# State space stage of a Macaron kernel: one transfer per repeated tile, and one overlapping read for the four shifted copies

## The chip, the cores and the metric

The kernel runs on one core of a Trainium2 chip. The core has TensorE (PE), VectorE (DVE), ScalarE (ACT), GpSimd (POOL) and SyncE (SP); here SP issues every transfer, in its program's order, to a queue that 16 DMA engines serve. Time is device microseconds of one execution. A profiled execution gives the span and the trace; single runs without a profile give the median that is compared.

## The reference

The input is `[16, 512, 256]` in float32: 16 sequences of 512 positions. Two layers follow each other. The first is a feed-forward part with blockwise FP4 rounding, a state space part, and the feed-forward part again. The second is a feed-forward part with a mixture of low-rank experts, causal attention with ALiBi, and the experts again. The change touches the state space part alone:

```python
xz = hidden_states @ W_in                       # 256 -> 2 x 512
x, z = jnp.split(xz, 2, axis=-1)
x = conv(x, conv_w)                             # 4 taps along the sequence, per channel
x = silu(x + conv_b)
proj = x @ W_x                                  # dt_low (16), B (16), C (16)
dt = jax.nn.softplus(dt_low @ W_dt + b_dt)      # 512 channels
A = -jnp.exp(A_log)                             # 512 x 16
...
h = jnp.exp(dt_t[..., None] * A) * h + (dt_t * x_t)[..., None] * B_t[:, None, :]
y = jnp.einsum('bds,bs->bd', h, C_t)
...
y = y + x * D
y = y * silu(z)
out = y @ W_out
```

There are 512 channels with 16 states each, for every sequence: 8192 recurrences of 512 steps.

## The kernel before

Three parts run one after the other: `ffn_phase` on all sequences, `mamba_phase` (the state space stage), then `ffn_phase` again and `attn_phase`. Only `mamba_phase` and its weights are touched.

**One scan.** VectorE runs the recurrence with one scan instruction (line 975) over a tile of 128 partitions by 2 x 512 elements. A partition is a pair of channel and state: 32 channels times 4 states, and the two halves of the free dimension are two further groups of 32 channels. So a sequence takes 32 scans: `where(t)` gives `b` (sequence), `c` (block of 128 channels, 0 to 3) and `k` (0 to 7, of which `k // 2` is one of four groups of states, `q`, and `k % 2` the half `p` of the channels). Each scan needs `da = exp(dt * A)` (ScalarE, `factors`), `bx = dt*u * B` (GpSimd, `make_bx`; for `q = 2` TensorE makes it instead, `turn_bx`), and after it `g = h * C` (VectorE or GpSimd), which TensorE sums over the states into `y` (`accumulate`).

**Repeated tiles.** `dt` and `dt*u` are made once per channel, on 128 partitions of channels, but the scans want each channel on four partitions (one for each state of a group), and `B` and `C` on 32 (one for each channel). This repetition is done through DRAM:

- `to_dtu` (line 762) writes the tile `dt` (dt and dt*u, two blocks of channels) to DRAM as `dd`. `fetch_steps(b, c)` (line 562) reads it back as two tiles `ds` (p = 0, 1), each 128 partitions by 2 x 2 x 512, in four transfers of 32 partitions, one for each repetition. `ds` has four buffers.
- `proj` holds B and C; two transfers (line 745) write them to DRAM as `bd`. `fetch(b, q)` (line 549) fills a tile `bc` with four transfers, each of which repeats one row of `bd` on 32 partitions.

**Shifted copies.** The convolution is done by TensorE from a stack `xs` of 128 partitions: four copies of 32 channels, each shifted by one more position. `to_xp` (line 661) copies the projected block to `xp`, stores it to DRAM as `xc` (line 679), and fills the stack with four transfers of 32 partitions, one for each tap, each with its own offset (line 682). The first three columns of the stacks were set to zero once (line 521). `taps(c)` (line 649) is the product that reads the stack. The first sequence does its convolution on VectorE, without a stack.

**Order.** `prepare(b + 1)` is a generator for all that the next sequence needs (projection, convolution, B, C, dt). The loop over `t` (line 959) runs a scan and its surrounding work and then advances `prepare` by one step, so the next sequence is prepared between the scans of the running one. Instructions of the compute engines in this stage are kept in program order (`keep_in_program_order`), so one that waits holds all that stand behind it on its engine. Fetches for the next block or sequence are issued at fixed places by `k` and `c` (lines 1012 to 1028).

## Time and profile before

| | us |
|---|---|
| median of 3 runs | 4369.89 (4368.17 to 4375.62) |
| profiled execution, its own time | 4368.95 |
| its span | 4367.2 |
| VectorE busy, whole span | 3630.1 (83%) |
| TensorE busy, whole span | 3748.3 (86%) |
| GpSimd busy, whole span | 1844.2 (42%) |

The DMA view lists the transfers by source and size; these are the ones that the change touches, with the median time from issue to landing:

| transfer | count | KB each | us to landing |
|---|---|---|---|
| `ds<-dd` | 512 | 256 | 6.5 |
| `xs<-xc` | 240 | 256 | 4.7 |
| `bc<-bd` | 256 | 128 | 6.3 |
| `dd<-dt` | 32 | 1024 | 4.7 |
| `xc<-xp` | 60 | 256 | 3.5 |

How to read it: a busy share over the whole span mixes stages with different limits, so the state space stage has to be read by itself, from windows of time. A transfer's time to landing includes its wait in the queue behind others that were issued before. "Released by" in a list of waits is the event that came last.

### The profile page before, as it was taken

Reading aid. Unit: us, or ns where it says so; the run is one execution under the profiler, and the core shown is the slowest. Engines: PE = TensorE matmul, PEld = TensorE weight load, DVE = VectorE, ACT = ScalarE, POOL = GpSimd, SP = SyncE. Lnnn points to the kernel's source line nnn. Section 1 sums busy time; section 2 is a strip of 40 time slices with the busy share of each in tenths; the row PEclk is TensorE's granted clock in tenths of the full one; section 3 lists DMA queues with packets and bytes.
Section 4 is the critical chain, followed back from the end, with each engine's and each line's share of the span. In section 5 each row is a group of like instructions: output and inputs, shape, how many; then the busy total and the mean of one; then the engine's idle time right before and its main releaser. Section 6 shows DMA issues by size and latency. Waiting matters only on the chain.

```text
span 4367.2 us, 68836 instructions
## 1 busy us (share of the span) xinstructions
PE 3748.3 (86%) x26498; PEld 2068.1 (47%) x26498; DVE 3630.1 (83%) x5002; ACT 2317.5 (53%) x3546; POOL 1844.2 (42%) x1687
## 2 busy tenths in 40 slices
PE   7999966777777777777777779999999999999989
PEld 4666632333333233333333346666764555555547
DVE  9999837887788888887878979999877888888876
ACT  4444336666666667766666634443534444444444
POOL 1000027888788788888888920000211111111122
PEclk9999978889888888898888889999999999999999
DMA  4000035667776666666677520000000000000002
GB/s 140 15 15 20 15 93 140 160 164 167 176 173 158 156 159 162 163 164 160 159 174 173 131 107 1 1 1 1 13 20 16 16 21 18 19 15 20 18 13 68
DMA packets 165786, 371.32 MB, mean 85 GB/s; under 512 B 37633, under 2 KB 57666, under 8 KB 165458
## 3 DMA queue, kind: packets, MB, share of 16 engines
q1 hardware_dynamic: 165458, 366.93, 33.3%
q8 instruction: 208, 3.41, 0.3%
q14 instruction: 120, 0.98, 0.1%
HBM read 272.18 MB, written 77.86 MB: 80 GB/s over the span
## 4 chain that ended last, share of the span: by engine, by line
PE 60%; DVE 15%; ACT 9%; DMA 9%; issue 3%; POOL 2%; SPq 2%; DVEq 0%; ACTq 0%; POOLq 0%
PE s L1192 10%; PE g L288 7%; PE u L288 7%; PE o L324 7%; DVE h L975 6%; DMA ds<-dd 5%; PE p L491 5%; PE p L1192 4%; PE y L491 4%; ACT da L482 3%; PE p L1195 3%; PE o L1192 3%; DMA xc<-xp 3%; PE da L491 2%; PE o L491 2%
## 5 line engine op out<-in xcount | busy, mean ns | idle before, releaser
L485 POOL TENSOR_TENSOR bx<-ds,bc 128x1024 f32<-128x1024 f32 x384 | 900.0, 2361 | 258.3 <-DMA ds<-dd 203.7
L482 ACT ACTIVATE da<-ds,a_neg 128x511 f32<-128x511 f32 x768 | 528.2, 689 | 285.4 <-DMA ds<-dd 103.8
L491 PE MATMUL y<-g,fold 128*32 128x512 f32 x2048 | 406.4, 673 | 185.0 <-DVE g L488 147.8
L485 POOL TENSOR_TENSOR g<-hs,bc 128x1024 f32<-128x1024 f32 x224 | 527.3, 2365 | 83.9 <-DVE hs L975 81.7
L975 DVE TENSOR_TENSOR_SCAN hs<-da,bx 128x1024 f32<-128x1024 f32 x224 | 508.1, 2279 | 65.6 <-POOL bx L485 65.1
L1363 ACT ACTIVATE eT<-s 128x768 f32<-128x768 f32 (+1 forms) x384 | 338.3, 881 | 420.9 <-PE s L1192 420.9
L1369 POOL TENSOR_SCALAR_AFFINE_SELECT eT<-eT 128x256 f32<-128x256 f32 (+1 forms) x384 | 189.0, 492 | 864.1 <-ACT eT L1363 864.1
L975 DVE TENSOR_TENSOR_SCAN h<-da,bx 128x1024 f32<-128x1024 f32 x160 | 366.8, 2292 | 127.1 <-POOL bx L485 77.9
L1192 PE MATMUL s<-k,q 32*128 32x256 f32 (+3 forms) x2048 | 459.5, 470 | 9.1 <-DVE mx L1323 5.7
L1323 DVE TENSOR_REDUCE mx<-s 128x2 f32<-128x1024 f32 (+3 forms) x512 | 410.2, 822 | 12.5
L975 DVE TENSOR_TENSOR_SCAN h<-ds,da 128x1024 f32<-128x1024 f32 x128 | 293.8, 2296 | 150.7 <-PE da L491 87.3
L1192 PE MATMUL s<-qm,k 32*128 32x512 f32 (+3 forms) x2048 | 385.7, 471 | 17.8 <-ACT eT L1363 11.4
L488 DVE TENSOR_TENSOR g<-h,bc 128x1024 f32<-128x1024 f32 x288 | 350.8, 1218 | 15.6 <-issue 0.4
L491 PE MATMUL p<-xT,w_in 128*128 128x512 f32 x500 | 293.9, 717 | 58.7 <-ACT dT L482 33.8
L1319 DVE TENSOR_TENSOR s<-s,mask 128x256 f32<-128x256 f32 (+1 forms) x384 | 198.8, 518 | 154.3 <-PE s L1192 143.9
L293 ACT ACTIVATE sl<-g 128x352 f32<-128x352 f32 x256 | 118.4, 464 | 384.9 <-PE g L288 373.7
L1192 PEld LDWEIGHTS s<-k,q 32*128 32x128 f32 x2048 | 206.3, 185 | 171.2 <-issue 93.6
L1520 POOL TENSOR_TENSOR g<-rs,v 128x4 f32<-128x4 f32 x64 | 13.1, 209 | 636.8 <-ACT rs L1517 549.4
L491 PEld LDWEIGHTS y<-g,fold 128*32 128x32 f32 x2048 | 60.5, 114 | 444.5 <-DVE g L488 253.9
L491 PE MATMUL da<-diag,dT 128*32 128x128 f32 x8192 | 247.8, 275 | 4.6 <-DVE hs L975 4.4
L491 PEld LDWEIGHTS da<-diag,dT 128*32 128x32 f32 x8192 | 217.8, 110 | 68.3 <-issue 45.2
L514 POOL MEMSET ds<- 128x2 f32 x2 | 0.1, 101 | 532.9 <-DMA xd<-x 532.9
(286 smaller groups left out, 7777.8 us busy)
## 6 DMA issues: line engine op xcount, KB each, us to landing
ds<-dd SPq DMA_DIRECT2D x512, 256.0 KB, 6.5
xs<-xc SPq DMA_DIRECT2D x240, 256.0 KB, 4.7
bc<-bd SPq DMA_DIRECT2D x256, 128.0 KB, 6.3
dd<-dt SPq DMA_DIRECT2D x32, 1024.0 KB, 4.7
xc<-xp SPq DMA_DIRECT2D x60, 256.0 KB, 3.5
x<-_attn_hidden_states_dram SPq DMA_DIRECT2D x16, 512.0 KB, 7.1
xd<-x SPq DMA_DIRECT2D x16, 512.0 KB, 2.6
xo<-xd SPq DMA_DIRECT2D x16, 512.0 KB, 3.7
```

Of the source, the lines that this page charges most:

```text
L288: nc.tensor.matmul(dst, lhsT=xT[:, k, c * P : (c + 1) * P], rhs=w[:, k, f0 : f0 + HF], start=(k == 0), stop=(k == KD - 1),)
L324: last = nc.tensor.matmul(o, lhsT=hT[:, f, :], rhs=wdT[:, f, :], start=(f == 0), stop=False)
L482: return tc.keep_in_program_order(nc.scalar.activation(out, in_, func, **kw))
L485: tc.keep_in_program_order(nc.gpsimd.tensor_tensor(out, in0, in1, op=op))
L488: tc.keep_in_program_order(nc.vector.tensor_tensor(out, in0, in1, op=op))
L491: tc.keep_in_program_order(nc.tensor.matmul(out, **kw))
L975: tc.keep_in_program_order(nc.vector.tensor_tensor_scan(flat(h), flat(da[t % 2]), flat(bx[t % 2] if turned else bx.pop(t)), 0.0, op0=ALU.m ...
L1192: tc.keep_in_program_order(nc.tensor.matmul(out, **kw))
L1319: nc.vector.tensor_tensor(own, own, const["mask"][:, :w].unsqueeze(1).to_broadcast([P, 2, w]), op=ALU.add)
L1323: nc.vector.tensor_reduce(mx[:, t, 2 * pair : 2 * pair + 2, RM], s[:, :, off : off + (t + 1) * P], axis=AX.X, op=ALU.max,)
L1363: const["exp"] = nc.scalar.activation(eT[:, 2 * pair : 2 * pair + 2, e0 : e0 + w], s[:, :, :w], AF.Exp)
L1369: nc.gpsimd.affine_select(out=own, in_=own, compare_op=ALU.is_ge, fill=0.0, base=0, pattern=[[0, 2], [0, n], [1, P]] if n > 1 else [[0, 2] ...
```

## The change

- `xp` gets three more columns on its left (`XS` = 515), set to zero once, so that `xc` in DRAM holds each channel's row with its zeros in front; `xc` is laid out with the channel `m` outermost and the four groups `i` next to each other.
- The stack is filled by one transfer, whose source is an access pattern written by hand: four copies, each starting one element later, of 32 rows of 2057 elements that run over all four groups. The stacks need no zeros of their own.
- `dd` is laid out by `[j, p, m, g, x, s]`, so that all that one `ds` tile needs of a channel is one run of 2048 elements. `to_dtu` writes it with four transfers of 64 partitions. A `ds` tile is filled by one transfer with the repetition of four as the outermost dimension of its source.
- A `bc` tile is filled by one transfer of four rows, each repeated 32 times.
- The transfers that fill the stack and that write `dd` are put on a list (`later`) and issued at the next step of the loop (`run_later`); the places of the fetches by `k` and `c` are written anew.

The instructions on SP, as built, per sequence: `ds` 8 where there were 32, `bc` 4 for 16, `xs` 4 for 16, `dd` 8 for 2. The access patterns as built (step and count of each dimension, outermost first):

```
ds  out [2048,128][1,1][1,2048]   in [0,4][2048,32][1,2048]      before: out [2048,32][1024,2][1,1024]  in [1024,32][32768,2][1,1024]
bc  out [1024,128][1,1][1,1024]   in [4096,4][0,32][1,1024]      before: out [1024,32][1,1024]          in [0,32][1,1024]
xs  out [2060,128][1,1][1,2057]   in [1,4][2060,32][1,2057]      before: out [2060,32][515,4][1,512]    in [512,32][16384,4][1,512]
xc  out [515,4][2060,32][1,515]   in [515,128][1,1][1,515]       before: out [512,128][1,512]           in [512,128][1,512]
dd  out [1024,2][2048,32][1,1024] in [2048,64][1,1][1,1024]      before: out [1024,128][131072,2][1,1024] in [2048,128][1024,2][1,1024]
```

```diff
+XS = SEQ + DCONV - 1
...
-            w["xp"].append(mw.tile([P, SEQ], F32, name=f"xp{i}"))
+            xp = mw.tile([P, XS], F32, name=f"xp{i}")
+            nc.gpsimd.memset(xp[:, : DCONV - 1], 0.0)
+            w["xp"].append(xp)
...
-                t = m1.tile([P, 4, SEQ + DCONV - 1], F32, name=f"xs{i}")
-                nc.gpsimd.memset(t[:, :, : DCONV - 1], 0.0)
-                stacks.append(t)
+                stacks.append(m1.tile([P, 4, XS], F32, name=f"xs{i}"))
...
-                    for i in range(4):
-                        n = 4 * i + q
-                        nc.sync.dma_start(
-                            out=bc[32 * i : 32 * i + 32],
-                            in_=bds[b][n : n + 1].to_broadcast([32, 2, SEQ]),
-                        )
-                        yield
+                    nc.sync.dma_start(
+                        out=bc,
+                        in_=bds[b].rearrange("(i q) x s -> q i (x s)", i=4)[q]
+                        .unsqueeze(1).to_broadcast([4, 32, 2 * SEQ]),
+                    )
...
-                        for i in range(4):
-                            nc.sync.dma_start(
-                                out=t[32 * i : 32 * i + 32],
-                                in_=rows_of[:, 2 * p : 2 * p + 2],
-                            )
-                            yield
+                        nc.sync.dma_start(
+                            out=t,
+                            in_=steps_of[b, c // 2][c % 2, p]
+                            .rearrange("m g x s -> m (g x s)")
+                            .unsqueeze(0).to_broadcast([4, 32, 4 * SEQ]),
+                        )
+                        yield
...
-                    act(xp, p, AF.Copy)
-                    xc = md.tile([4, 32, SEQ], F32, name="xc", tag="xc", bufs=4)
-                    nc.sync.dma_start(out=xc.rearrange("i m s -> (i m) s"), in_=xp)
-                    for k in range(DCONV):
-                        o = DCONV - 1 - k
+                    act(xp[:, DCONV - 1 :], p, AF.Copy)
+                    xc = md.tile([32, 4, XS], F32, name="xc", tag="xc", bufs=4)
+                    nc.sync.dma_start(out=xc.rearrange("m i s -> i m s"), in_=xp)
+
+                    def spread_x():
+                        n = 4 * XS - DCONV + 1
                         nc.sync.dma_start(
-                            out=stacks[c % 2][32 * k : 32 * k + 32, :, o : o + SEQ],
-                            in_=xc.rearrange("i m s -> m i s"),
-                        )
+                            out=stacks[c % 2].rearrange("p i s -> p (i s)")[:, :n],
+                            in_=bass.AP(
+                                xc.tensor, xc.offset, [[1, DCONV], [4 * XS, 32], [1, n]]
+                            ),
+                        )
+
+                    later.append(spread_x)
...
-                    dd = md.tile([2, P, 2, SEQ], F32, name="dd", tag="dd", bufs=4)
-                    nc.sync.dma_start(out=dd.rearrange("j p x s -> p j x s"), in_=t)
+                    dd = md.tile([2, 2, 32, 2, 2, SEQ], F32, name="dd", tag="dd", bufs=4)
                     steps_of[b, h] = dd
+
+                    def store():
+                        for j in range(2):
+                            for p in range(2):
+                                nc.sync.dma_start(
+                                    out=dd[j, p].rearrange("m g x s -> g m (x s)"),
+                                    in_=t[64 * p : 64 * p + 64, j],
+                                )
+
+                    later.append(store)
...
+            def run_later():
+                for do in later:
+                    do()
+                later.clear()
...
+                run_later()
                 for _ in range(2 if t < 8 or s in (24, 26, 28, 30) else 1):
                     next(rest if t < 4 else ahead, None)
...
+                if b and s == 0:
+                    fetch(b, NQ - 1)
+                if k == (0, 0, 0, 2)[c]:
+                    steps = fetch_steps(*divmod(b * NDC + c + 1, NDC))
+                    next(steps, None)
+                if k == (1, 3, 2, 3)[c]:
+                    next(steps, None)
                 if c == NDC - 1 and k in (2, 4, 6):
-                    for _ in fetch(b + 1, k // 2 - 1):
-                        pass
-                if b and s == 0:
-                    for _ in fetch(b, NQ - 1):
-                        pass
+                    fetch(b + 1, k // 2 - 1)
```

More of the change, by code (lines that the diff above doesn't have):

```diff
@@ L519, in mamba_phase @@
             for i in range(2):
-                t = m1.tile([P, 4, SEQ + DCONV - 1], F32, name=f"xs{i}")
-                nc.gpsimd.memset(t[:, :, : DCONV - 1], 0.0)
-                stacks.append(t)
+                stacks.append(m1.tile([P, 4, XS], F32, name=f"xs{i}"))
             state, xns, xos, zss, rows, norms, bds = {}, {}, {}, {}, {}, {}, {}
-            spread, steps_of = {}, {}
+            spread, steps_of, later = {}, {}, []
             h0 = ps_h.tile([P, 2, SEQ], F32, name="h", tag="h")
@@ L553, in fetch @@
                     rows[b, q] = bc
-                    for i in range(4):
-                        n = 4 * i + q
-                        nc.sync.dma_start(
-                            out=bc[32 * i : 32 * i + 32],
-                            in_=bds[b][n : n + 1].to_broadcast([32, 2, SEQ]),
-                        )
-                        yield
+                    nc.sync.dma_start(
[3 more added lines that the diff above has]
+                    )
             def fetch_steps(b, c):
                 if b < NB:
-                    rows_of = steps_of[b, c // 2][c % 2].rearrange(
-                        "(g m) x s -> m g x s", m=32
-                    )
                     for p in range(2):
@@ L932, in mamba_phase @@
                     break
-            for _ in itertools.chain(
-                fetch_steps(0, 0), *(fetch(0, q) for q in range(NQ))
-            ):
-                pass
+            run_later()
+            for _ in fetch_steps(0, 0):
+                pass
+            for q in range(NQ):
+                fetch(0, q)
             spare.clear()
@@ L991, in mamba_phase @@
                     next(stat, None)
+                run_later()
                 for _ in range(2 if t < 8 or s in (24, 26, 28, 30) else 1):
@@ L1011, in mamba_phase @@
                     finish_mult(*done.pop())
-                if c == NDC - 1 and k in (2, 4, 6):
-                    for _ in fetch(b + 1, k // 2 - 1):
-                        pass
-                if b and s == 0:
-                    for _ in fetch(b, NQ - 1):
-                        pass
-                if c < NDC - 1:
-                    if k == 0:
-                        steps = fetch_steps(b, c + 1)
-                    for _ in range((4, 0, 0, 2, 2, 1)[k] if k < 6 else 0):
-                        next(steps, None)
-                else:
-                    if k == 2:
-                        steps = fetch_steps(b + 1, 0)
-                    if k in (2, 3, 4, 5):
-                        next(steps, None)
-                        next(steps, None)
+                if b and s == 0:
[5 more added lines that the diff above has]
+                    next(steps, None)
+                if c == NDC - 1 and k in (2, 4, 6):
+                    fetch(b + 1, k // 2 - 1)
                 if s == STEPS - 1:
```

## The prediction

> **What bounds the kernel now.** I first read the page's slices, to place the stage that changes. The rows are forty equal slices of 109 us.
>
> ```profile
> DMA  4000035667776666666677520000000000000002
> GB/s 140 15 15 20 15 93 140 160 164 167 176 173 158 156 159 162 163 164 160 159 174 173 131 107 1 1 1 1 13 20 16 16 21 18 19 15 20 18 13 68
> ```
>
> The state space stage is the stretch from slice 5 to slice 23, the only one where transfers are busy for long. Next came the table of windows, cut into stretches of 120.8 us, which is the distance between equal points of neighbouring sequences (one sequence of 512 is 32 scans). Columns: busy time of each engine, granted clock, share of the 16 DMA engines that is busy, GB/s.
>
> ```profile
> core 0: us, PE busy (x) PEld busy (x) DVE busy (x) ACT busy (x) POOL busy (x), PEclk, DMA share, GB/s
> 820.80:941.60 120.80, 91.14 (x832) 38.92 (x830) 99.11 (x73) 81.31 (x115) 98.70 (x58) 0.87 0.68 169
> 941.60:1062.40 120.80, 91.75 (x832) 38.84 (x826) 100.07 (x72) 83.31 (x117) 97.94 (x57) 0.92 0.68 166
> 1062.40:1183.20 120.80, 91.01 (x818) 38.73 (x816) 96.67 (x70) 79.88 (x112) 97.97 (x57) 0.86 0.66 161
> ```
>
> VectorE and GpSimd carry some 99 us of the 121, TensorE 91; the DMA engines rest for a third, about 40 us. No engine is full, so I read the chain of waits over the stage (607 to 2545 us), where the transfers show:
>
> ```profile
> by line: DVE h L975 12.9%; DMA ds<-dd 11.6%; PE p L491 11.4%; PE y L491 8.4%; ACT da L482 7.3%; DMA xc<-xp 5.7%; PE da L491 5.4%; issue 4.3%; DVE g L488 3.8%; PE o L491 3.7%; DVE hs L975 3.4%; ACT L482 3.1%; SPq L682 1.9%; ACT zs L482 1.5%;
> ```
>
> Of 1938 us, `ds<-dd` holds 225, `xc<-xp` 110 and SP's issuing of `xs` 37: transfers already sit on the path, so how fast they run decides. For that I read the DMA view in four short windows. In order: `xs` and `ds` (1031.1 to 1040.2 us); `ds` and `bc` (1106.7 to 1133.5); one `dd<-dt` store (1214.8 to 1217.7); reloads of whole x tiles (2570.2 to 2572.2).
>
> ```profile
> DMA packets 815, 1.84 MB, mean 202 GB/s; under 512 B 111, under 2 KB 111, under 8 KB 815
> q1 hardware_dynamic: 815, 1.84, 96.0%
> ...
> DMA packets 1921, 6.05 MB, mean 226 GB/s; under 512 B 448, under 2 KB 448, under 8 KB 1919
> q1 hardware_dynamic: 1919, 6.03, 94.6%
> ...
> DMA packets 272, 1.05 MB, mean 362 GB/s; under 512 B 16, under 2 KB 16, under 8 KB 272
> q1 hardware_dynamic: 272, 1.05, 90.2%
> ...
> DMA packets 215, 0.82 MB, mean 408 GB/s; under 512 B 16, under 2 KB 16, under 8 KB 215
> q1 hardware_dynamic: 215, 0.82, 99.9%
> ```
>
> The percentage is the busy share of sixteen engines, so the rate of one busy engine follows. Loads into 32 partitions: 202/(16 x 0.960) = 13.2 and 226/(16 x 0.946) = 14.9 GB/s, together about 14. The store from 128 partitions: 362/(16 x 0.902) = 25.1. Loads into 128 partitions: 408/16 = 25.5. One more thing is in the third row: 272 packets, 16 of them tiny, for 128 rows of two 4 KB pieces, so 256 and one closing packet for each of 16 engines. Every large transfer of this trace has an outermost count of 128 or 32, which deals out evenly to 16.
>
> **The change, part by part.** The instructions of TensorE, VectorE and ScalarE, and their order, stay the same. Only SP's queue changes, and two memsets of GpSimd (110 ns each), which move ahead of the stage into work on weights; they count as nothing, and 0.2 us without that cover.
>
> Issues on SP, per sequence: `ds` 32 to 8, `bc` 16 to 4, `xs` 16 to 4, `dd` 2 to 8, so 42 fewer. At 0.43 us (the middle of the `ds` and `xs` issues) that is 18 us less of SP time, of which the path holds about 37/16 = 2 us.
>
> Bytes per sequence: `ds` 8 x 128 rows x 8192 B = 8.39 MB, `bc` 4 x 128 x 4096 = 2.10, `xs` 4 x 128 x 8228 = 4.21, `xc` 4 x 128 x 2060 = 1.05, `dd` 8 x 64 x 4096 = 2.10, and `xo`, `xe`, `xn`, `bd` 1.64 as before. The volume hardly moves. What moves is the shape. The DRAM side of a new `ds`, `bc` or `xs` transfer is four copies of 32 rows, with the four outermost; the DRAM side of `xc` is now four groups of 32 rows; that of a `dd` store is two groups of 32. No transfer of before has an outermost count of 4 or 2, so the trace prices it from two sides only. At one end the rows are still dealt to 16 engines, and a whole tile of 128 partitions runs like the x reloads, at 408 GB/s. At the other end one engine moves one outermost group: four engines work on `ds`, `bc`, `xs`, `xc`, and two on `dd`. I take the second end, since sixteen engines could share four groups only by cutting them, and no transfer in the trace shows that.
>
> [...] No run here shows a count of 4.
>
> With the second end and shared low engines, the two engines that also serve `dd` carry, per sequence:
> - loads: 8.39/4 + 2.10/4 + 4.21/4 + 1.64/16 = 3.77 MB
> - stores: 1.05/4 + 2.10/2 = 1.31 MB
>
> The rate of one engine when only four run is the second unknown. Bounds: 14 GB/s (a block of 32 partitions as destination) and 25.3 (whole tiles). I take 14 for loads, because each engine's share is again one block of 32 partitions, and 25.1 for stores, from the `dd` row itself. Then 3.77/14 = 269 us and 1.31/25.1 = 52 us, 321 us of work on one engine where a sequence lasts 121 us today.
>
> [...]
>
> All the scans and matmuls (99 us on the fullest engine) can hide below that, but not wholly: SP's queue is in order and its `xs` waits for `xc` to land (155 us in the window 700 to 2300 us, the second line below), and nothing behind it is issued: the next `ds`, the next `xc`, `xe`.
>
> ```profile
> SPq L679 <- ACT xp L482: 195.5, 39, 7.3
> ...
> SPq L682 <- DMA xc<-xp: 155.4, 52, 6.5
> ...
> SPq L572 <- DMA dd<-dt: 52.4, 14, 5.2
> ```
>
> Of the 40 us in which the DMA engines rest today I keep half, 20 us (bounds 0 and 40). A sequence then takes 341 us, 220 more. Who waits: `taps` on TensorE needs the whole of `xs`; behind it in TensorE's order stand `turn_bx` and the sums into y, and so the scans of the running sequence, whose `ds` buffers come free late, and SP stops on those. A tile of `ds` alone takes 1.05/4/14 = 19 us, where its four quarters now land in 6.5 us each.
>
> Fifteen sequences are prepared in the loop: 15 x 220 = 3300 us. Ahead of the first scan stand the first `dd`, two `ds` and four `bc`: 8 x 0.131/25.1 + 2 x 19 + 4 x 9.4 = 117 us, against 21 now (first `bc` issued at 607.7 us, first `bx` at 628.2), so 96 more. The last sequence fetches only six `ds` (112 us, hidden). Deferring `xs` and `dd` to the next step costs a scan's 3.8 us each time, inside the 321. Sum: 3400 us on a profiled execution of 4368.95 us (its span is 4367.2), which is 0.9 us below the median of the runs: about **7760 us**.
>
> **The rivals.**
> - Engine rate. Four engines on blocks that lie 32 partitions apart may not get in each other's way, since the 13 to 15 GB/s was read with sixteen engines on one block. At 25.3 GB/s: 5.08/25.3 = 201 us, with 20 of rest 221; 15 x 100 + 63 at the start (the 117 at this rate, less 21) = 1560 more: 5930 us. For it: x reloads reach 25.5 on every engine. Against: all loads to 32 partitions at a time stay near 14.
> - Stores as slow as loads, more rest. `dd` reads 32 partitions per engine: 5.08/14 = 363 us, 40 of rest, 15 x 282 + 130 at the start = 4360 more: 8730 us. For it: the block shape holds for stores too. Against: the `dd` row of before ran at 25.1.
> - The other side: the groups are cut to sixteen engines after all. Then a tile lands in 1.05 MB/408 GB/s plus about 2 us, 4.6 us instead of quarters that queue for 6.5 to 8.8. Half of the 225 and 110 us in the chain goes, with 25 of SP's 37: 190 less, 4180 us. It decides as soon as more than about ten engines serve a `ds`. For it: every counted packet row closes with 16. Against: all of those had counts that divide.
> - Nothing measurable, within 0.2% (what runs of this kernel can tell from no change): the gain of whole tiles would have to cancel the wait for the slower `dd`. I find no row for such a balance.
>
> **How the numbers follow.** Forecast (confined, loads at 14) 0.50; confined at full rate 0.25; confined with slow stores 0.18; spread and faster 0.06; no change 0.01. The confined cases are all slower, 0.93. The range reaches from 5700 (full rate, less rest than I keep) to 8900 (slow stores, more rest), which leaves out the spread case and some of the tails.
>
> **What would show it.** Right: a mean DMA rate in the stage that falls from 165 to some 60 GB/s, with a DMA share between two and four sixteenths; `ds` landing in about 20 us or more behind others, near 1024 KB each; `bx`, `da` and `p<-xs` waiting on `ds` and `xs` for most of the stage; the same busy times on the compute engines; the later stages unchanged. Wrong: `ds` of 1024 KB landing within 8 us, or a DMA share above 0.4 in the stage (more engines at work); a stage of 220 us per sequence at a per-engine rate near 25 would convict the rate, not the confinement.

## The result, and the profile after

| | before | after |
|---|---|---|
| median of 4 runs each, same chip (us) | 4372.76 (4368.17 to 4377.07) | 6106.06 (6101.14 to 6114.0) |
| ratio, with its 95% interval | 1 | 1.3966 [1.3942, 1.399] |
| span of the profiled execution (us) | 4367.2 | 6106.5 |
| first scan begins, last scan begins (us) | 630.6, 2541.1 | 652.9, 4277.5 |
| time per sequence, from the first scan of sequence 2 to that of sequence 14, counted from 0 (us) | 119.7 | 232.2 |
| from the last scan's begin to the end (us) | 1826 | 1829 |

The table places the loss. Fifteen sequences take 15 x (232.2 - 119.7) = 1688 us more, the start takes 22 more, and the ends of the stage some 26 more: 1736 of the 1739 us. The last 3 us lie behind the stage, and the parts before and after it hardly moved.

The page's slices of after, each 152.7 us (rows: busy tenths of TensorE, its granted clock in tenths, mean busy share of the 16 DMA engines, GB/s):

```profile
span 6106.5 us, 67831 instructions
PE   7998244344443443443453453454999999999999
PEclk9999576676676776776776776676999999999999
DMA  3000222222222222222222222222200000000001
GB/s 104 18 14 24 87 74 87 85 77 90 82 80 93 82 81 92 81 81 89 83 81 88 84 82 87 85 82 79 77 1 1 9 15 20 17 19 18 17 12 56
DMA packets 110259, 371.57 MB, mean 61 GB/s; under 512 B 21537, under 2 KB 41570, under 8 KB 85874
```

Slices 4 to 28, counted from 0, are the state space stage. Its rate fell from about 165 GB/s to 82, and the busy share from 6 or 7 tenths to 2: the transfers are slower and yet most engines rest. The bytes are those of before, as its own line of totals shows:

```profile
DMA packets 165786, 371.32 MB, mean 85 GB/s; under 512 B 37633, under 2 KB 57666, under 8 KB 165458
```

Compare the packets under 512 B. The prediction read 16 tiny ones at the end of a `dd` store, one for each of 16 engines. If every large transfer ends so, and is dealt to as many engines as its outermost count has groups, after has fewer of them by: `ds` 512 x 16 - 128 x 4 = 7680, `bc` 256 x 16 - 64 x 4 = 3840, `xs` 240 x 16 - 60 x 4 = 3600, `xc` 60 x 16 - 60 x 4 = 720, `dd` 32 x 16 - 128 x 2 = 256. The sum is 16096, and 37633 - 21537 = 16096. So a count of 4 is served here by four engines and a count of 2 by two, to the packet.

Windows of one sequence each, in after (columns as in the prediction):

```profile
core 0: us, PE busy (x) PEld busy (x) DVE busy (x) ACT busy (x) POOL busy (x), PEclk, DMA share, GB/s
1003.00:1235.00 232.00, 101.83 (x850) 43.47 (x842) 101.04 (x71) 81.37 (x115) 100.18 (x59) 0.69 0.24 85
1235.00:1467.00 232.00, 92.62 (x737) 36.12 (x736) 96.62 (x70) 76.52 (x110) 91.06 (x55) 0.66 0.25 84
1467.00:1699.00 232.00, 101.34 (x825) 42.22 (x822) 98.88 (x70) 82.14 (x115) 98.81 (x59) 0.68 0.24 84
```

VectorE and GpSimd do their 91 to 101 us nearly as before, but the sequence lasts 232. A share of 0.24 is 0.24 x 16 = 3.84 engines, and 85/3.84 = 22 GB/s for each. By the prediction's byte counts, and if all kinds share their engines, the two that also serve `dd` carry 3.77 + 1.31 = 5.08 MB per sequence, the next two 4.03, and the other twelve 1/16 of 1.64 each. At 22 GB/s, 5.08 MB is 231 us (an estimate, since it gives every engine the mean rate). The trace's records of single packets do not name an engine, but they show how many packets are in flight at a time, which stands here for the engines at work, from 700 to 4200 us: none for 4.8% of the time, two for 12%, four for 68%, six or more for 3.5%. That fits kinds of transfer that share the same engines, and not kinds that spread over different fours. No engine at work for 4.8% leaves the fullest two at most 221 of the 232 us for their 5.08 MB, so they run at 23 GB/s or more and rest for 11 us or more. With what queues on them they set the time of the stage.

The chain of work that ended last, followed through 900 to 2100 us of after, goes through those transfers:

```profile
by line: DMA xc<-xp 29.4%; DMA xs<-xc 16.4%; DMA ds<-dd 14.4%; SPq L774 8.0%; PE p L494 5.6%; POOL bx L488 4.7%; DVE h L992 4.2%; POOL g L488 3.3%; issue 2.6%; ACT L485 2.1%; DVE hs L992 1.7%; PE y L494 1.5%; PE da L494 1.5%; ACT da L485 1.
```

Who waits is in the list of waits of after (engine, line, what it waited for: us in total, times, longest):

```profile
PE p L494 <- DMA xs<-xc: 926.3, 60, 49.4
...
POOL bx L488 <- DMA bc<-bd: 534.5, 30, 18.6
...
ACT L485 <- DMA ds<-dd: 448.0, 15, 29.9
...
POOL bx L488 <- DMA ds<-dd: 390.7, 18, 38.5
```

Every one of the 60 stacks holds TensorE up, by 15 us on average; before, TensorE waited 17.7 us for `xs` in all, and `bx` 1.4 us for `bc`. TensorE's matmul `p<-xs,cwd` has a median of 1061 ns where it had 593, in a stage whose granted clock is 0.66 to 0.69 instead of 0.86 to 0.92. TensorE's busy time in all grew by 126 us (3748.3 to 3874.2); whether any of that lies on the path was not tried.

SP waits for `xc` to land before it can issue `xs`, as the prediction said, and far longer than the 174.1 us of the whole kernel before:

```profile
SPq L680 <- DMA xc<-xp: 1298.8, 60, 28.9
```

SP also stops where it waits for nothing. Its instructions in the trace (start, us, line and transfer, how many):

```profile
1084.94 4.69 SPq L555 DMA_DIRECT2D bc<-bd  x1
1089.69 20.14 SPq L774 DMA_DIRECT2D dd<-dt  x3
...
1110.88 14.65 SPq L555 DMA_DIRECT2D bc<-bd  x2
1125.63 14.35 SPq L567 DMA_DIRECT2D ds<-dd  x2
```

These are not waits for a semaphore, but the issuing itself: three stores take 20 us, where the five kinds of issue had medians of 0.34 to 0.43 us before, 2.1 at the longest. Over the kernel the `dd` issues of line 774 have a median of 2.05 us and a longest of 15.7, those of `bc` 4.73 and 10.8, those of `ds` 0.54 and 14.9. All issues of the five kinds add up to 1236 us, where they took 482 before. The chain that ended last puts 5% of the kernel's span on the `dd` issues.

### The profile page after: what moved, and what is told of

It is laid out like the page before. It is cut to its first block, busy times and chain, and to the rows that moved or that the text cites. A ratio compares the mean times of both kernels' runs of the same rounds, so it can differ in the third digit from the quotient of the medians.

```text
span 6106.5 us, 67831 instructions
## 1 busy us (share of the span) xinstructions
PE 3874.2 (63%) x26498; PEld 2109.7 (35%) x26498; DVE 3641.1 (60%) x5002; ACT 2315.8 (38%) x3546; POOL 1843.8 (30%) x1687
## 2 busy tenths in 40 slices
DMA packets 110259, 371.57 MB, mean 61 GB/s; under 512 B 21537, under 2 KB 41570, under 8 KB 85874
## 4 chain that ended last, share of the span: by engine, by line
PE 38%; DMA 34%; DVE 9%; SPq 5%; POOL 5%; ACT 5%; issue 2%; DVEq 0%; POOLq 0%; ACTq 0%
DMA xc<-xp 16%; DMA xs<-xc 10%; DMA ds<-dd 7%; PE s L1202 7%; PE g L289 5%; PE u L289 5%; SPq L774 5%; PE o L325 5%; PE p L494 3%; PE p L1202 3%; DVE h L992 3%; POOL bx L488 3%; PE p L1205 2%; PE o L1202 2%; POOL g L488 2%
## 5 line engine op out<-in xcount | busy, mean ns | idle before, releaser
L488 POOL TENSOR_TENSOR bx<-ds,bc 128x1024 f32<-128x1024 f32 x384 | 897.7, 2355 | 1258.0 <-DMA bc<-bd 534.5
L494 PE MATMUL p<-xs,cwd 128*32 128x512 f32 x480 | 116.3, 1057 | 926.3 <-DMA xs<-xc 926.3
L485 ACT ACTIVATE u<-p,cb 128x512 f32<-128x512 f32 x60 | 41.3, 688 | 1013.4 <-PE p L494 1013.4
L494 PE MATMUL p<-xT,w_in 128*128 128x512 f32 x500 | 343.1, 823 | 90.3 <-ACT dT L485 65.6
L641 PE MATMUL p<-ident,xn 128*128 128x128 f32 x120 | 40.5, 440 | 537.9 <-ACT xT L485 513.5
L494 PEld LDWEIGHTS p<-xs,cwd 128*32 128x32 f32 x480 | 14.0, 140 | 985.4 <-issue 985.4
```

Source lines behind the costliest of these rows:

```text
L485: return tc.keep_in_program_order(nc.scalar.activation(out, in_, func, **kw))
L488: tc.keep_in_program_order(nc.gpsimd.tensor_tensor(out, in0, in1, op=op))
L494: tc.keep_in_program_order(nc.tensor.matmul(out, **kw))
```

## The experiments

Each is after with the edit shown, if nothing else is said. A transfer is called cut when it is issued in pieces whose outermost count is 16 or 32.

**m1_rates.** Transfers alone, with no computation: one tile of 128 x 8192 B from DRAM, filled in several shapes, each between two whole-tile transfers.

```python
def copies4():
    nc.sync.dma_start(out=dst, in_=src[:32].unsqueeze(0).to_broadcast([4, 32, W]))
def copies2_far():
    nc.sync.dma_start(out=dst, in_=src[:64].unsqueeze(0).to_broadcast([2, 64, W]))
def copies2_near():
    nc.sync.dma_start(out=dst[:64], in_=src[:32].unsqueeze(0).to_broadcast([2, 32, W]))
def quarters(order):
    for i in order:
        nc.sync.dma_start(out=dst[32 * i : 32 * i + 32], in_=src[:32])
...
def rows16():
    nc.sync.dma_start(out=dst, in_=src[:16].unsqueeze(1).to_broadcast([16, 8, W]))
```

> Leaves the whole computation out: the output is ones, and only transfers between one DRAM tile of 1 MB and one SBUF tile of 128 x 2048 run, one kind after the other, each waiting for the one before. It measures the rate of one DMA engine by shape. Theory A (a transfer is dealt by the outermost count; a block of 32 partitions takes some 220 GB/s whoever writes it): the whole tile on 16 engines some 2.5 us of data at 400 GB/s and 16 closing packets; four copies of 32 rows some 10 us at 105 GB/s and 4 closing packets; two copies of 64 rows 20 us at 52 GB/s; four quarters of 32 rows, dealt to 16 engines, 4.7 us at 220 GB/s; eight copies of 4 rows into 32 partitions the same 200 GB/s as sixteen engines. Rival (an engine has 14 GB/s whenever its destination is a block of 32 partitions): four copies 19 us at 55 GB/s, eight engines into 32 partitions 110 GB/s. Two copies of 32 rows into partitions 0 to 63: 52 GB/s if blocks 32 apart don't hinder each other, 28 if they do; two loads of 64 rows on 16 engines: 400 GB/s if they don't, 220 if they do.

The DMA view in the window of each shape, in the order `copies4`, `copies2_far`, `copies2_near`, quarters in the order 0, 1, 2, 3, quarters in the order 0, 2, 1, 3, `rows16`; then two halves of 64 rows on 16 engines, and four blocks of 32 rows, each filled by eight engines:

```profile
DMA packets 132, 1.05 MB, mean 60 GB/s; under 512 B 4, under 2 KB 4, under 8 KB 4
q1 hardware_dynamic: 132, 1.05, 23.4%
...
DMA packets 130, 1.05 MB, mean 50 GB/s; under 512 B 2, under 2 KB 2, under 8 KB 2
...
DMA packets 66, 0.52 MB, mean 33 GB/s; under 512 B 2, under 2 KB 2, under 8 KB 2
...
DMA packets 192, 1.05 MB, mean 202 GB/s; under 512 B 64, under 2 KB 64, under 8 KB 64
...
DMA packets 192, 1.05 MB, mean 210 GB/s; under 512 B 64, under 2 KB 64, under 8 KB 64
...
DMA packets 144, 1.05 MB, mean 223 GB/s; under 512 B 16, under 2 KB 16, under 8 KB 16
...
DMA packets 160, 1.05 MB, mean 206 GB/s; under 512 B 32, under 2 KB 32, under 8 KB 32
...
DMA packets 160, 1.05 MB, mean 184 GB/s; under 512 B 32, under 2 KB 32, under 8 KB 32
q1 hardware_dynamic: 160, 1.05, 48.1%
```

The tiny packets again count the engines: 4, 2, 2, four times 16 (twice), 16, twice 16, four times 8. Two engines on blocks 64 partitions apart reach 25 GB/s each, on blocks 32 apart 16.5. Four engines on four neighbouring blocks reach 15 each, close to the 14 that the prediction took. So two engines hindered each other here on neighbouring blocks and not on blocks two apart; why was not shown. The last shape is against the prediction's reason for 14 GB/s: eight engines that write one block of 32 partitions move 184/(16 x 0.481) = 24 GB/s each, so a block alone does not hold an engine to 14. The quarters, with sixteen engines at once on a block, moved 202/(16 x 0.905) = 14 for each (a busy share of 90.5% in their window). In the packet records a packet of 8 KB took 309 ns in the median with these eight engines and in `copies2_far`, and some 600 in `copies4` and the quarters. Of the two expectations, the first missed the four copies (10 us), its rival the eight engines (110 GB/s). Quarters in the order 0, 2, 1, 3 run a little faster, and `rows16`, one transfer for a tile, is barely faster than quarters. Timed from the first packet of the data to the last, the quarters took 5.06 and 4.80 us. A lone transfer of four copies, then, took 17.4 us, but after ran at 22 GB/s per engine, not at 15: the rate was still open.

**e1_all16.** All five kinds of transfer cut, with the layouts of DRAM, `later` and the places of the fetches as in after.

```diff
-                    nc.sync.dma_start(
-                        out=bc,
-                        in_=bds[b].rearrange("(i q) x s -> q i (x s)", i=4)[q]
-                        .unsqueeze(1).to_broadcast([4, 32, 2 * SEQ]),
-                    )
+                    for i in range(4):
+                        n = 4 * i + q
+                        nc.sync.dma_start(
+                            out=bc[32 * i : 32 * i + 32],
+                            in_=bds[b][n : n + 1].to_broadcast([32, 2, SEQ]),
+                        )
...
-                            out=t,
-                            in_=steps_of[b, c // 2][c % 2, p]
-                            .rearrange("m g x s -> m (g x s)")
-                            .unsqueeze(0).to_broadcast([4, 32, 4 * SEQ]),
+                                out=t[32 * i : 32 * i + 32],
+                                in_=steps_of[b, c // 2][c % 2, p],
...
-                    nc.sync.dma_start(out=xc.rearrange("m i s -> i m s"), in_=xp)
+                    for i in range(4):
+                        nc.sync.dma_start(
+                            out=xc[:, i, :], in_=xp[32 * i : 32 * i + 32]
+                        )
...
-                            out=stacks[c % 2].rearrange("p i s -> p (i s)")[:, :n],
-                            in_=bass.AP(
-                                xc.tensor, xc.offset, [[1, DCONV], [4 * XS, 32], [1, n]]
-                            ),
+                                out=stacks[c % 2][32 * k : 32 * k + 32].rearrange(
+                                    "p i s -> p (i s)"
+                                )[:, :n],
+                                in_=bass.AP(
+                                    xc.tensor, xc.offset + k, [[4 * XS, 32], [1, n]]
+                                ),
...
-                                    out=dd[j, p].rearrange("m g x s -> g m (x s)"),
-                                    in_=t[64 * p : 64 * p + 64, j],
+                                    o = 64 * p + 32 * g
+                                    nc.sync.dma_start(
+                                        out=dd[j, p][:, g], in_=t[o : o + 32, j]
+                                    )
```

> The changed kernel with its layouts, its list of deferred transfers and its places of the fetches, but every confined transfer cut so that its outermost count is 32: ds, bc and xs in four transfers, xc in four, dd in sixteen per sequence. Theory 1 (the loss is the confinement to the two or four lowest engines): a sequence takes 118 to 126 us again, the kernel 4330 to 4470 us. Theory 2 (the loss is what the change does to the order: the deferral by a step, the places of the fetches, xs waiting for all of xc): above 5000 us.

Measured: 4338.08 us (4335.97 to 4343.74), ratio to before 0.9912 [0.9897, 0.9927]; 117.0 us per sequence. The waits of this kernel in the stage (700 to 2300 us), and behind them the two of before in the same stretch:

```profile
PE p L494 <- DMA xs<-xc: 62.1, 28, 7.0
...
POOL bx L488 <- DMA ds<-dd: 24.6, 4, 6.5
...
PE p L491 <- DMA xs<-xc: 8.7, 4, 6.3
...
POOL bx L485 <- DMA ds<-dd: 169.5, 32, 7.5
```

The whole loss is gone, and 0.9% more: what the change kept is slightly better than before. So the loss is not in the layouts, the deferral or the places of the fetches. All of the 1768 us between after and this kernel goes with the cutting, which changes the number of engines and the number of transfers; `e6_bc_one16` below separates these two for `bc`.

**e2_ds16, e3_dd16, e4_xs16, e5_bc16.** After with one part alone cut: the second hunk above (`ds`), the last (`dd`), the third and fourth (`xc` and `xs`), the first (`bc`).

> The changed kernel with ds alone cut into four transfers of 32 partitions (16 engines). The load theory (the work of the lowest engine, 201 us per sequence at 25.3 GB/s, sets the time): 83 us leave that engine and 20 to 37 come back as its sixteenth, so a sequence falls from 230 to 165 to 190 us, the kernel to 5100 to 5500 us. The chain theory (the way xp to xc to xs to taps sets it, DMA xc 21% and xs 13% of the chain in the stage): ds matters only where xc and xs stand behind it, 5400 to 5900 us.

> The changed kernel with the dd stores alone cut into 32 rows (16 engines). The load theory: engines 0 and 1 lose 1.05 MB each (42 us), the four low engines are then even at 159 us; a sequence 190 to 200 us, the kernel 5500 to 5650 us. The chain theory (xc and xs set the time): less than 200 us won, above 5900 us. Issues of dd on SP, up to 5 us each now, fall to 0.5.

> The changed kernel with xc and xs alone cut into four transfers each (16 engines). The load theory: the low engines lose 1.31 MB (52 us) and get 12 to 23 back; a sequence 190 to 200 us, the kernel 5500 to 5650 us. The chain theory: the waits of taps for xs (926 us in all) and of SP for xc (1299 us) go for the most part, 4800 to 5300 us. If xc and xs still queue behind ds on the low engines, the gain is that of the load theory or less.

> The changed kernel with bc alone cut into four transfers of 32 partitions (16 engines). The load theory: 0.52 MB (21 us) leave the low engines and 5 to 9 come back; a sequence 215 us, the kernel 5850 to 5950 us. The chain theory: bx waits 534 us for bc in all; the start of a sequence comes earlier by up to 18 us, 5800 to 6000 us. No theory expects more than 350 us.

| cut | time (us) | less than after | less per sequence | MB taken off each of the fullest engines, per sequence | us per MB |
|---|---|---|---|---|---|
| `ds` | 5504.08 | 602 | 37.6 | 8.39 x (1/4 - 1/16) = 1.57 | 24 |
| `dd` | 5724.16 | 382 | 23.4 | 2.10 x (1/2 - 1/16) = 0.92 | 25 |
| `xc`, `xs` | 5796.64 | 309 | 21.4 | 5.26 x (1/4 - 1/16) = 0.99 | 22 |
| `bc` | 5938.53 | 168 | 10.5 | 2.10 x (1/4 - 1/16) = 0.39 | 27 |

The gain goes with the load that each takes off the fullest engines, 22 to 27 us per MB, so it is the load that decides; the bytes moved do not order it, since `dd` and `bc` move 2.10 MB each and `dd` brings twice as much. But at 22 GB/s a MB is 45 us, and the times of `ds`, `dd` and `xs` lie 4, 74 and 147 us above what the load theory expected. The chain theory, by which `xc` and `xs` carried the loss, is off by some 500 us for `e4_xs16` and by 180 for `e3_dd16`; `e2_ds16` and `e5_bc16` lie in its ranges too and do not separate the two. In `e4_xs16` what was expected for a queue behind `ds` came in, a gain below that of the load theory. Its waits show that a cut transfer still has to queue:

```profile
PE p L494 <- DMA xs<-xc: 650.0, 45, 33.8
...
POOL bx L488 <- DMA bc<-bd: 540.2, 32, 18.8
...
ACT L485 <- DMA ds<-dd: 447.9, 15, 29.9
```

A stack that comes in sixteenths is only complete when the sixteenths of the fullest engines are, and these stand behind `ds`, `bc` and `dd`. The four gains add up to 1461 of 1768 us, so the parts also help each other. That this is why a MB buys only about half of its 45 us is argued from these waits, not shown. A second reason is in the windows of `e2_ds16` and `e4_xs16`:

```profile
900.00:3000.00 2100.00, 1066.76 (x8840) 441.43 (x8832) 1065.50 (x758) 882.51 (x1242) 1043.98 (x612) 0.72 0.38 101
...
900.00:3000.00 2100.00, 957.99 (x8179) 406.18 (x8177) 982.93 (x697) 803.46 (x1129) 968.09 (x565) 0.71 0.34 93
```

A busy engine moves 101/(16 x 0.38) = 17 GB/s in both (93/(16 x 0.34) in the second), not 22. The pieces that sixteen engines write to one block ran at 14 in `m1_rates`; by that the sixteenth that comes back costs more than its bytes. How much each reason takes was not told apart. In `e3_dd16` the `dd` issues of SP are back at a median of 0.42 us, 0.59 at most, but a `ds` issue there still takes up to 16.1 us. So stores on two engines are not alone in stopping SP; loads on four do it too.

**e6_bc_one16.** e1_all16, and `bc` filled by one transfer on 16 engines: every row of `bd` is stored four times, the columns of `W_x` are put in another order, so that 16 rows, each repeated 8 times, make a tile.

```diff
-                    for i in range(4):
-                        n = 4 * i + q
-                        nc.sync.dma_start(
-                            out=bc[32 * i : 32 * i + 32],
-                            in_=bds[b][n : n + 1].to_broadcast([32, 2, SEQ]),
-                        )
+                    nc.sync.dma_start(
+                        out=bc,
+                        in_=bds[b][4 * q : 4 * q + 4].rearrange("i r x s -> (i r) (x s)")
+                        .unsqueeze(1).to_broadcast([16, 8, 2 * SEQ]),
+                    )
...
-                bd = md.tile([NS, 2, SEQ], F32, name="bd", tag="bd")
+                bd = md.tile([NS, 4, 2, SEQ], F32, name="bd", tag="bd")
```

> As e1_all16, but bc is one transfer per tile on 16 engines: bd is stored with every row of B and C four times (two stores with a repeated source, in an order of states made by a permutation of W_x's columns), so that a bc tile is 16 rows, each repeated 8 times, on 128 partitions. Theory 1 (only the engine count counts, and whole tiles run at some 400 GB/s): bc lands in about 3 us alone instead of four that share 220 GB/s; 0 to 80 us less than e1_all16, as the queue is full for 27 us of each sequence where the bc stand. Theory 2 (a tile that comes in one transfer is what costs): slower than e1_all16 by more than 50 us.

Measured: 4339.4 us, ratio 0.9912 [0.9895, 0.9928], the same as `e1_all16`. One `bc` transfer per tile costs nothing by itself here, where it is dealt to 16 engines (`rows16`, of the same form, closes with 16 tiny packets), and it brings nothing either; 12 fewer issues per sequence change nothing that shows. `rows16` of `m1_rates`, at 223 GB/s against 202, leaves little to win.

**e7_ds_one16.** e6_bc_one16, and `dd` stored in four copies, so that a `ds` tile is one transfer on 16 engines.

```diff
-                            in_=t[o : o + 32, j]
+                            in_=t[o : o + 32, j].rearrange("m x s -> m (x s)")
+                            .unsqueeze(1).to_broadcast([32, 4, 2 * SEQ]),
...
-                        for i in range(4):
-                            nc.sync.dma_start(
-                                out=t[32 * i : 32 * i + 32],
-                                in_=steps_of[b, c // 2][c % 2, p],
-                            )
+                        nc.sync.dma_start(
+                            out=t,
+                            in_=steps_of[b, c // 2][c % 2, p].rearrange(
+                                "i m g x s -> (i m) (g x s)"
+                            ),
+                        )
```

> As e6_bc_one16, and ds is one transfer per tile on 16 engines too: the dd stores write four copies (8.4 MB per sequence in place of 2.1), so that a ds tile is 128 rows of 8 KB in DRAM. Theory 1: still at the level of before, 4280 to 4500 us: loads of ds at 400 instead of 220 GB/s save 17 us of transfers per sequence, and the stores cost 15 to 30 more. Theory 2 (whole tiles in one transfer cost): above 4700 us.

Measured: 4617.01 us, ratio 1.0546 [1.053, 1.0562], between the two expectations and in neither. Its transfers (KB each, median us from issue to landing):

```profile
dd<-dt SPq DMA_DIRECT2D x256, 512.0 KB, 8.9
ds<-dd SPq DMA_DIRECT2D x128, 1024.0 KB, 11.3
...
bc<-bd SPq DMA_DIRECT2D x64, 512.0 KB, 16.2
```

A `ds` tile lands no sooner, and `bc` needs 16.2 us where `e6_bc_one16` has 4.7: the stores now move four times the bytes (475 MB in all against 375); that what is issued behind them waits for this is argued. How much of the 278 us is due to the bytes and how much to the stores' place in the queue was not told apart.

**m2_lag.** Transfers alone. Why 22 GB/s per engine in the kernel and 15 in `m1_rates`? A transfer of four copies ran alone, then three back to back, then both again behind two small transfers, meant to delay some of the engines by different times.

```python
def stagger():
    nc.sync.dma_start(out=side[96:113, :480], in_=src[:17, :480])
    nc.sync.dma_start(out=side[64:67], in_=flat[:3])
```

> Leaves the whole computation out, as m1_rates. A transfer of four copies of 32 rows (1 MB) ran at 60 GB/s alone and at over 100 GB/s in places of the changed kernel. Theory A (blocks 32 partitions apart hinder each other only while two engines walk them in step; a lag of one group of 4 partitions, 32 KB, between the engines of a pair frees both): alone 17 us at 60 GB/s; three queued back to back without a wait some 50 us at 60 GB/s, as the step is kept; behind a transfer of 17 rows (which one engine takes) and one of 3 rows of 32 KB (engines 0 to 2), so that each pair is 32 KB out of step, one transfer takes 10 to 13 us, and three back to back some 31 to 35 us at 90 to 105 GB/s. Rival B (a backlog alone frees them): three back to back 30 us with and without the lag. Rival C (the source, four engines on the same bytes, is what is slow): 60 GB/s in all four cases.

The GB/s in forty slices of each window, first the three without the delay (36.2 us), then the three with it (34.4 us), each with its totals:

```profile
GB/s 72 72 72 72 36 81 63 72 54 63 63 72 63 81 81 81 81 100 100 91 109 109 109 109 100 100 109 109 109 109 100 109 109 109 109 100 109 109 63 18
DMA packets 396, 3.15 MB, mean 87 GB/s; under 512 B 12, under 2 KB 12, under 8 KB 12
...
GB/s 68 19 10 29 57 48 105 114 105 105 105 105 114 105 105 95 114 114 105 105 95 114 114 105 105 95 114 114 105 95 105 114 114 105 95 105 114 105 38 38
DMA packets 410, 3.20 MB, mean 93 GB/s; under 512 B 16, under 2 KB 25, under 8 KB 25
```

Four engines that started together ran at about 70 GB/s together. Left to themselves in a backlog they ran mostly at 100 to 109 after some 15 us; behind the two small transfers they ran at 95 to 114 after some 5 us, from the same source rows. The two closed with four tiny packets together (16 in that window, where three transfers of four have 12), which fits the one engine and the three of the expectation; which engines these are no record shows. The packet records fit a slow loss of step: in the first of the three, packets take 309 or some 610 ns, the engines close it at 62.3, 62.7, 63.4 and 63.8 us, and from 66 us on nearly all packets take 309 to 318. That a pair of engines on neighbouring blocks hinders each other only in step is a reading that both ways out of it support and that no row shows; no delay but this one was run, so the 32 KB and the 4 partitions of the expectation stay an assumption. Three without the delay took 36 us, where by the expectation a step that is kept would have taken some 50: that half of the theory fell. A lone transfer ran at 66 GB/s; behind the delay its whole window, small transfers included, has 74, and its middle 88 to 132. The kernel lies between: in after, the window with one `xs` and the `xc` behind it, on a queue that begins empty (1002.4 to 1022 us), has 68 GB/s, and a backlog of `ds` and `bc` (1110 to 1140 us) 91:

```profile
DMA packets 263, 1.33 MB, mean 68 GB/s; under 512 B 6, under 2 KB 6, under 8 KB 134
...
DMA packets 543, 2.73 MB, mean 91 GB/s; under 512 B 16, under 2 KB 16, under 8 KB 404
```

**e8_no_defer.** e1_all16 without the list `later`: the stack and the stores of `dd` are issued where they are made.

```diff
-                    later.append(spread_x)
+                    spread_x()
...
-                    later.append(store)
+                    store()
```

> e1_all16 (4338 us, 0.9912 of before) without the list of deferred transfers: xs and dd are issued where they are made. Theory 1 (the deferral is what e1_all16 gains over before, since SP's in-order queue no longer stands at xs or dd while a ds could go): 4360 to 4390 us. Theory 2 (the gain is from the rows of 8 KB and from the places of the fetches): within 0.3% of e1_all16.

Measured: 4334.4 us (4321.46 to 4337.95), ratio 0.9916 [0.9899, 0.9934], as `e1_all16`. The deferral neither costs nor brings anything that shows. Whether the layouts or the places of the fetches bring the 0.9% was not tried.

**e9_order.** e1_all16 with the quarters issued in the order 0, 2, 1, 3.

```diff
-                    for i in range(4):
+                    for i in (0, 2, 1, 3):
```

This stands at `bc` and at `ds`, and with `k` at `xs`.

> e1_all16 with the four quarters of ds, bc and xs issued in the order 0, 2, 1, 3, so that neighbours in the queue lie 64 partitions apart: 218 against 207 GB/s in m1_rates. If the transfers' rate still holds the path in places: 5 to 20 us less than e1_all16; if it is hidden: within 0.3%.

Measured: 4314.45 us (4311.65 to 4320.51), ratio 0.9878 [0.9863, 0.9893]. This is the fastest kernel of the study, 1.2% below before and, by the ratios, 0.3% below `e1_all16`: the gain that was expected if the rate still holds the path in places. `ds` lands in 5.3 us where `e1_all16` has 5.7, and `p` waits 54.4 us for `xs` in the stage instead of 62.1. It fits the 5.06 and 4.80 us of `m1_rates`: quarters that follow each other in the queue no longer lie on neighbouring blocks.

**e10_before_bc4.** The kernel before, with `bc` alone as one transfer of four rows.

```diff
-                    for i in range(4):
-                        n = 4 * i + q
-                        nc.sync.dma_start(
-                            out=bc[32 * i : 32 * i + 32],
-                            in_=bds[b][n : n + 1].to_broadcast([32, 2, SEQ]),
-                        )
-                        yield
+                    nc.sync.dma_start(
+                        out=bc,
+                        in_=bds[b].rearrange("(i q) x s -> q i (x s)", i=4)[q]
+                        .unsqueeze(1).to_broadcast([4, 32, 2 * SEQ]),
+                    )
+                    yield
```

> The kernel before with bc alone made one transfer per tile (outermost count 4), nothing else of the change. Load theory: the lowest engines carry 0.52 MB more and a sixteenth of the rest, 17.4/16 = 1.09 MB, 1.61 MB in a sequence of 120 us, so at 14 to 25 GB/s 64 to 115 us: they don't become the bound, but bc lands late at the turn of a sequence by 10 to 20 us: 4450 to 4650 us. If only a saturated low engine cost anything: within 0.5% of before.

Measured: 4573.52 us, ratio 1.047 [1.0452, 1.0487], 203 us more than before, within the load theory's range. The waits of this kernel, then the same of before:

```profile
POOL bx L485 <- DMA ds<-dd: 389.3, 49, 30.1
...
ACT da L482 <- DMA ds<-dd: 174.5, 26, 21.8
...
POOL bx L485 <- DMA ds<-dd: 203.7, 38, 11.7
...
ACT da L482 <- DMA ds<-dd: 103.8, 18, 7.6
```

The transfer that was changed is `bc`; the one that is late is `ds`, which is still dealt to 16: of the packets under 512 B, 37633 - 33793 = 3840 are gone, those of `bc` alone (`bx` waits 17.1 us for `bc`). Four engines get 2.10/4 = 0.52 MB per sequence from `bc` instead of 0.13. By the packet records, from 700 to 2300 us, exactly four packets are in flight for 13% of the time, where before it was 0.5%; that the `ds` quarters wait for their shares on these four engines is argued from that. None is in flight for 21% of the time, so a load that is unevenly spread cost 203 us here though no engine was full.

## Why the prediction was right and wrong

- **The confinement** was the first of its two unknowns, and it took the right end: the 16096 missing closing packets and `e1_all16` show it. Its sum also took it that all kinds share the same low engines, which no run had shown; in after four packets were in flight for 68% of the time, two for 12% and six or more for 3.5%, which fits shared engines, and since no record names an engine, which ones they are (the "low" and "lowest" ones, or those with numbers, of the prediction and the expectations) no run shows. The rival of a spread to all engines falls as a reading of after; what a spread gives is 4338 us, or 4314 in the better order, where that rival worked out 4180. It counted a gain from whole tiles. `e6_bc_one16` shows none for `bc`; `e7_ds_one16` shows none for `ds` either, but pays for its tiles with four times the stores.
- **The rate** is the step that failed: "I take 14 for loads, because each engine's share is again one block of 32 partitions". That reason does not hold: eight engines on one block run at 24 GB/s each in `m1_rates`. A lone transfer of four copies does run at 15, close to 14, but with one engine on a block: `m1_rates` has two engines at 16.5 each on neighbouring blocks and at 25 on blocks two apart, and in `m2_lag` four reach up to 27 each in a backlog. In the kernel the mean over loads and stores was 22, and the two fullest engines did their 5.08 MB in at most 221 us, where the prediction had 321.
- **The rest** that was kept, 20 us, was 11 by the time in which no engine is at work. So of the 109 us between 341 and 232, some 100 belong to the rate and some 9 to the rest.
- **The start** was put at 96 us more and measured at 22. It was worked out at the slow rate, with all four `bc` and eight `dd` stores ahead of the first scan; in after only four stores are issued there (SP's line 774 at 610.87 us, the next four at 666.42).
- **The sum.** The misses are 15 x 220 against 1688, which is 1612 us, and 74 at the start, less 29 at the ends of the stage and beyond, which had no term: 1657 us. The prediction's own terms add up to 4368.95 + 3396 + 0.9 = 7766 us, which it gave as about 7760; the 6106 measured are 1660 less, so 3 us are left to rounding and the spread of the runs. That this lies in the stated range is owed to its lower end, drawn down to the rival with the full rate.
- **Nearest** came that rival, "Engine rate" (5930 us): 25.3 GB/s with 20 us of rest, 221 per sequence. Its time of the fullest engine, 201 us, is some 20 us too short and its rest 9 too long, so the two errors offset each other in part. It held that sixteen engines on one block say little about four engines on four blocks. That was right for a backlog (25 to 27 GB/s each after some 15 us in `m2_lag`), and wrong for transfers that start together (15 in `m1_rates`).
- **Stores as slow as loads** (8730 us) falls: the stage as a whole ran at 22.
- **Who waits** was right for the product of the stack, first of all, and for `bx` and `da` on `ds`, and so was SP's wait for `xc`. The 534.5 us for which `bx` waits for `bc` were not named. The mean rate fell to 82 GB/s, not to some 60. Right were the unchanged volume, the later stages, a DMA share of 0.24, and the busy times of VectorE, ScalarE and GpSimd (3641.1 against 3630.1, 2315.8 against 2317.5, 1843.8 against 1844.2 us). The test that was named for the rate is the one that came in: near 220 us per sequence at a rate not far below 25.
- **Not foreseen**: that SP stops in the issuing itself. The prediction gave SP 18 us less of it per sequence; with 1236 us in place of 482 it was 47 more. The sum comes out without a term for it; whether it has a share of its own was not tried.

## What to carry to other kernels

The smaller of the outermost counts of a transfer's two sides said here how many DMA engines serve it (2, 4, 8 and 16 were seen, with 16 for counts of 32 and 128), and the tiny closing packets in the trace count them: a repetition of four put outermost made a whole tile a transfer for four engines, and in this stage, with transfers on the path, those few engines then set its time (the kernel took 40% longer with all of them so, and 4.7% with the 512 KB tiles alone). Fewer transfers gained nothing by themselves where it was tried, for `bc`. If pieces have to be cut, let neighbours in the queue go to blocks 64 partitions apart; that was worth 0.3% here and cost nothing.

## What the runs showed of the hardware

- Two engines on neighbouring blocks of 32 partitions ran at 16.5 GB/s each, on blocks 64 apart at 25. Eight engines on one block ran at 24 each, sixteen at 14. Four that started together on four neighbouring blocks ran at 15 (all `m1_rates`); in a backlog they reached 27 after some 15 us without any change in the program (`m2_lag`).
- With transfers confined to two or four engines, issuing one stopped SP for up to 15.7 us (`dd`) or 14.9 (`ds`), with no semaphore in it, where the medians before were 0.34 to 0.43 us.
- The clock granted to TensorE fell to 0.66 to 0.69 in the stage, in which it was busy for 0.4 to 0.44 of the time; before, it was 0.86 to 0.92 at 0.75. Which of the two leads to the other was not tried.
